# Keys and slots of chunk pairs by seven products, and weight sums kept in DRAM, in a float32 macaron block

## The chip, the cores and the metric

The kernel runs on one core of a Trainium2 chip. The metric is device time in microseconds of one execution. The profile is of one further execution of the same program; its times are counted from the start of its span.

The engines are called TensorE (PE in the profile), VectorE (DVE), ScalarE (ACT), GpSimd (POOL) and SyncE (SP). Each works through its own instructions in order. SP's queue issues nearly all transfers here, one behind the other; POOL's queue issues the indirect ones.

## The reference

The input is 2 batches of 1024 tokens with 512 features, all in float32. A mixture of two experts, an attention with slots and the mixture again are each added to the tokens:

```python
x = x + 0.5 * _L0_ffn_ref(_layernorm(x), w_router, w_fc, w_proj)
x = x + _L0_attn_ref(_layernorm(x), Wq, Wk, Wv, Wg, Ws, Wo, g_norm_weight)
x = x + 0.5 * _L0_ffn_ref(_layernorm(x), w_router, w_fc, w_proj)
# mixture: the router picks one of 2 experts for each token;
#   h = x @ w_fc[e].T  (2048 wide);  a = square(where(h >= 0, h, h / 2));  a @ w_proj[e].T * weight
# attention, 16 heads, 64 slots a head:
#   q, k = x @ Wq, x @ Wk (64 a head);  v, g = x @ Wv, x @ Wg (128 a head)
#   s = clip(x @ Ws, -32, 32);  z = cumulative logsumexp of s over the tokens;  p = exp(s - z)
#   hk = hk * exp(z_before - z) + k p^T;  ok = q hk;  u = softmax(ok)
#   hv = hv * exp(z_before - z) + p v^T;  o = u hv
#   o = o * rsqrt(mean(o^2) + eps) * g_norm_weight * silu(g);   o @ Wo
```

## The kernel before, in words

**Stages.** The first mixture runs from 0 to about 505 us, attention to about 1940, the last mixture to the end. A scheduler orders each engine's instructions and sets the semaphores. Tiles come from pools: `large` has 11 buffers of 8 KB in each partition and holds expert weights, attention weights and tokens; `sums` has 6 buffers of the same size. A load waits until an older tile's buffer is free, and everything behind it on SP's queue waits too.

**Mixture.** Tokens are sorted by expert through DRAM, then worked on in six passes of 2, 4, 2, 4, 1 and 4 tiles of 128 tokens (the last mixture: 4, 4, 4, 2, 2, 1). A pass takes the hidden layer in four quarters (`ck`), each with 1 MB of `w_fc` (tile `wfc`, L223) and 1 MB of `w_proj` (`wp`). The passes of four tiles use Strassen's seven products (matmuls L588 and L653); for these POOL makes sums of the weights, `S` (L538 to L541) and `R` (L550 to L553). The small passes multiply directly (L499 and L708), and there POOL only has its scatter transfers (L628). Finished tokens are scattered to DRAM by POOL's queue.

**Attention.** There are 2 batches × 4 groups of 4 heads × 8 chunks of 128 tokens = 64 units. Three neighbouring units are in work at a time, called `cur`, `mid` and `old`. For `cur` the loop projects keys and slots: `keys_slots` multiplies the chunk with `[Wk | Ws]` in four matmuls of 512 columns (L862) into one PSUM bank; ScalarE copies the key half (L871), VectorE clips the slot half (L873), ScalarE takes its exponential (L874). Then keys and slots are transposed (`tk`, L953 and L954), copied to `kET`, and the scores `Ap` computed (L966). VectorE masks them into `A` (L970), makes the running sum `CT` (L983) and its reciprocal `rC` (L988). In the next step of the loop `ok` uses `A` (L995 and L1000), and on it hang the softmax, the slot weights `Bp`, the output `ov`, the norm with a root on ScalarE (L1075), POOL's gating (L1079) and the output projection `po` (L1113). ScalarE's root and exponential need different tables, which it loads in between.

**Values and gates** of a pair of chunks already come from seven products (`values_gates`, L888), spread over the loop in four steps by `project_ahead`. The token sums `X` of the pair are made by VectorE (L905 to L908). The weight sums `G` are made by POOL in `group_sums` (L846 to L852), eight operations for each batch and group, during the units of the group before. One of the weights is overwritten by its sum.

**Weights.** `group_weights` and `value_gate_weights` load 1 MB each of `wks`, `wv`, `wg`, `wo` and 0.5 MB of `wq` for each batch and group.

## Time and profile before

| | |
|---|---|
| median of 3 runs | 2412.27 us (2410.39 to 2414.95) |
| the profiled execution's own time | 2413.41 us |
| its span | 2411.5 us |
| its mean granted TensorE clock | 0.994 |
| TensorE busy | 2350.5 us (97%) |
| VectorE, ScalarE, POOL busy | 1343.7, 757.7, 488.3 us |
| keys and slots, L862 | 512 passes of 128x512 |
| values and gates, L888, and `hU`, L588 | 10% and 6% of the chain that ended last |

Busy times come from the page. A float32 matmul is recorded as two passes, so four matmuls of a unit are eight records. The recorded duration of a pass includes an end that is modelled, and neighbouring passes overlap; how fast the stream runs is read from the distance of the starts in the timeline. "idle before" in a group's row is the idle time of that engine just before it, with the one that ended it. In the list of waits the numbers are us in total, how many times, and the longest.

### The profile page before, as it was taken

The page shows a single profiled execution, that of the slowest core. Times are in us where ns is not written, and L with a number is a line of the kernel's source. Part 1 is how long each engine was busy: PE and PEld are TensorE (multiplying, and loading weights), DVE is VectorE, ACT ScalarE, POOL GpSimd, SP SyncE. Part 2 cuts the span into 40 slices and gives each one's busy share as a digit, 9 for nine tenths or more (in the row PEclk, how much of TensorE's full clock was granted, in tenths as well). Part 3 has the DMA queues.
Part 4 walks back from the last instruction along what each step waited for, and adds up shares of the span by engine and source line. Part 5 has one row for each costly group of instructions (what it writes and reads, how often), then busy time and mean ns, then how long its engine had stood idle before and what let it go on. Part 6 is the DMA issues. An engine that isn't in the chain of part 4 may idle for free.

```text
span 2411.5 us, 27003 instructions
## 1 busy us (share of the span) xinstructions
PE 2350.5 (97%) x10168; PEld 1497.3 (62%) x10168; DVE 1343.7 (56%) x3020; ACT 757.7 (31%) x1408; POOL 488.3 (20%) x415
## 2 busy tenths in 40 slices
PE   6899999999999999999999999999999999999998
PEld 5587787855555555555555555555555568888865
DVE  5553455665645545556655645645646666766411
ACT  1222222223333333334433333333333332222222
POOL 3522415400100100100201100100102223644000
PEclk9999999999999999999999999999999999999999
DMA  7614335130100100100310100100001113313442
GB/s 262 232 53 178 109 111 204 56 143 1 62 18 1 62 18 1 49 22 14 109 37 36 47 33 1 47 32 1 26 1 53 53 53 122 137 62 131 157 170 96
DMA packets 37601, 180.66 MB, mean 75 GB/s; under 512 B 4575, under 2 KB 4575, under 8 KB 21088
## 3 DMA queue, kind: packets, MB, share of 16 engines
q1 hardware_dynamic: 31904, 161.58, 18.6%
q0 software_dynamic: 5280, 16.85, 1.8%
q8 instruction: 80, 1.31, 0.2%
q10 hardware_dynamic: 288, 0.52, 0.1%
q14 instruction: 49, 0.40, 0.1%
HBM read 160.50 MB, written 18.95 MB: 74 GB/s over the span
## 4 chain that ended last, share of the span: by engine, by line
PE 85%; DVE 7%; issue 4%; DMA 1%; POOL 1%; ACT 1%; SPq 0%; POOLq 0%; ACTq 0%; DVEq 0%
PE U L888 10%; PE po L1113 9%; PE pks L862 9%; PE oa L653 7%; PE hU L588 6%; PE o L653 5%; PE pq L944 5%; PE V L888 4%; PE hp L499 4%; PE op L708 3%; PE hV L588 3%; PE ok L1000 3%; PE C L888 2%; PE ok L995 2%; PE ov L1064 2%
## 5 line engine op out<-in xcount | busy, mean ns | idle before, releaser
L1079 POOL TENSOR_TENSOR sg<-sg,ms 128x512 f32<-128x512 f32 x64 | 67.7, 1058 | 1167.7 <-DVE ms L1077 1143.0
L862 PE MATMUL pks<-wks,xnT 128*128 128x512 f32 x512 | 264.9, 623 | 0.0
L1113 PE MATMUL po<-wo,oT 128*128 128x512 f32 x512 | 231.2, 593 | 1.0 <-ACT oT L1106 1.0
L499 PE MATMUL hp<-xsT,wfc 128*128 128x256 f32 (+1 forms) x768 | 150.9, 352 | 7.5 <-DVE t L486 4.4
L1113 PEld LDWEIGHTS po<-wo,oT 128*128 128x128 f32 x512 | 92.0, 190 | 92.9 <-issue 90.4
L499 PEld LDWEIGHTS hp<-xsT,wfc 128*128 128x128 f32 x768 | 128.6, 193 | 31.0 <-issue 10.0
L708 PE MATMUL op<-wp,a 128*128 128x512 f32 x320 | 143.2, 593 | 0.0
L1118 DVE TENSOR_TENSOR x<-po,x 128x512 f32<-128x512 f32 x64 | 44.2, 691 | 151.5 <-PE po L1113 151.5
L486 DVE SCALAR_TENSOR_TENSOR t<-hp,r 128x256 f32<-128x256 f32 (+1 forms) x96 | 36.3, 378 | 155.6 <-ACT r L485 152.2
L862 PEld LDWEIGHTS pks<-wks,xnT 128*128 128x128 f32 x512 | 83.0, 190 | 54.9 <-issue 46.2
L944 PE MATMUL pq<-xnT,wq 128*128 128x512 f32 x256 | 112.5, 592 | 0.0
L988 DVE RECIPROCAL rC<-CT 128x256 f32<-128x256 f32 x64 | 111.7, 1745 | 0.3
L588 PE MATMUL hU<-xsT,wfc 128*128 128x256 f32 x384 | 101.4, 386 | 2.0 <-ACT e L595 2.0
L895 ACT COPY u<-U 128x512 f32<-128x512 f32 x64 | 37.2, 581 | 197.0 <-PE U L888 197.0
L708 PEld LDWEIGHTS op<-wp,a 128*128 128x128 f32 x320 | 59.7, 190 | 60.9 <-issue 57.4
L1075 ACT ACT_TABLE_LOAD x59 | 75.7, 1283 | 61.8 <-DVE ms L1074 61.6
L871 ACT COPY k<-pks 128x256 f32<-128x256 f32 x64 | 23.8, 372 | 191.3 <-PE pks L862 183.2
L588 PEld LDWEIGHTS hU<-xsT,wfc 128*128 128x128 f32 x384 | 73.2, 193 | 16.0 <-issue 3.3
L1064 PEld LDWEIGHTS ov<-v,B 128*128 128x128 f32 x512 | 76.5, 191 | 10.1 <-issue 3.3
L485 ACT ACTIVATE r<-hp 128x256 f32<-128x256 f32 (+1 forms) x96 | 33.3, 347 | 156.2 <-PE hp L499 153.7
L925 ACT COPY v<-U 128x512 f32<-128x512 f32 x32 | 18.7, 585 | 201.8 <-PE U L888 201.8
L874 ACT ACT_TABLE_LOAD x63 | 80.8, 1283 | 1.1
(277 smaller groups left out, 4947.5 us busy)
## 6 DMA issues: line engine op xcount, KB each, us to landing
wfc<-in_w_fc_dram SPq DMA_DIRECT2D x48, 1024.0 KB, 4.9
wp<-in_w_proj_dram SPq DMA_DIRECT2D x48, 1024.0 KB, 6.5
wv<-in_w_v_dram SPq DMA_DIRECT2D x8, 1024.0 KB, 4.9
wg<-in_w_g_dram SPq DMA_DIRECT2D x8, 1024.0 KB, 4.9
wks<-in_w_ks_dram SPq DMA_DIRECT2D x8, 1024.0 KB, 4.8
wo<-in_w_o_dram SPq DMA_DIRECT2D x8, 1024.0 KB, 4.8
xs<-xs SPq DMA_DIRECT2D x6, 1032.0 KB, 7.0
wq<-in_w_q_dram SPq DMA_DIRECT2D x8, 512.0 KB, 3.6
```

Of the source, the lines that this page charges most:

```text
L499: m.mark = nc.tensor.matmul(hp, lhsT=wfc[:, dc * HQ + hc * P : dc * HQ + (hc + 1) * P], rhs=xT[:, dc, :], start=(dc == 0), stop=(dc == DC ...
L588: m.mark = nc.tensor.matmul(bank, lhsT=left[:, d, :], rhs=right[:, d, :], start=start and d == 0, stop=d == 1, skip_group_check=True,)
L653: nc.tensor.matmul(bank[:, t, :], lhsT=left(q)[:, ts(t, P)], rhs=right(q), start=first and q == 0 and (t == 0 or last), stop=last and q == ...
L708: nc.tensor.matmul(ops[j], lhsT=a[hc][:, ts(j, P)], rhs=wp[:, ts(hc, D)], start=(ck == 0 and hc == 0), stop=(ck == NHQ - 1 and hc == HQ // ...
L862: nc.tensor.matmul(pj, lhsT=xT[u.blk][:, dc, ts(u.c % 4, P)], rhs=w[:, ts(dc, 512)], start=(dc == 0), stop=(dc == DC - 1),)
L874: nc.scalar.activation(u.E, u.E, AF.Exp)
L888: nc.tensor.matmul(bank, lhsT=left[:, d, :], rhs=right(d), start=start and d == 0, stop=d == 1, skip_group_check=True,)
L944: nc.tensor.matmul(pj, lhsT=u.wq[:, c0 : c0 + P], rhs=xT[u.blk][:, dc, :], start=(dc == 0), stop=(dc == DC - 1),)
L988: nc.vector.reciprocal(u.rC, u.CT)
L1064: nc.tensor.matmul(op[:, h, :], lhsT=u.Bm[:, h % 2 * NPR + pr, :], rhs=u.v[:, ts(h, DV)], start=(u.c == 0), stop=(u.c == 0 or h % 2 == 1),)
L1075: nc.scalar.activation(ms, ms, AF.Sqrt, bias=eps, scale=1.0 / DV)
L1113: nc.tensor.matmul(pj, lhsT=u.oT[:, h, :], rhs=u.wo[:, ts(h, D)], start=(h == 0), stop=(h == HG - 1),)
```

## The change

*Keys and slots* are now computed for two chunks together. With the tokens as the left 2x2 block matrix (two chunks by two halves of the features) and the weights as the right one (two halves of the features by keys and slots), seven products of 256 columns take the place of eight. `keys_slots` is a generator: five products in the first step of an even unit, one each in its second and third (`next(keys)`). Two halves `U` and `V` of one PSUM bank (`kU`) accumulate, and one product has a bank of its own (`kC`). The partial results are copied by ScalarE and added by VectorE. The token sums are those of the values (`token_sums`). `project_ahead` for the values moves to odd units, with its last two of five steps in even ones; its `V` products come earlier.

*Weight sums* for values and gates (four operations for each group and half) and for keys and slots (four for each group) are made once, by POOL, in the first mixture's small passes (`weight_sums`, five or ten of its steps within a quarter). They are loaded for that, stored to DRAM (`vg_sums`, `ks_sums`) and loaded in attention for each batch and group like weights, in the units `c` = 4 to 7 of the group before. `group_sums` is gone.

*The tile of blank rows* moves from a constant to a sum tile, set in each mixture. *The last mixture* loads its first tokens before its first `wfc`, and its first `wp` after their preparation (`load_outer`).

```diff
-            self.wp0 = load_expert(w_proj, self.ex[0], 0, f"wp{ph}_0_0")
-            self.raw0 = self.load_tokens(0)
+            if self.split:
+                self.wfc0 = load()
+                self.load_outer()
+                self.raw0 = self.load_tokens(0)
+            else:
+                self.raw0 = self.load_tokens(0)
+                self.wfc0 = load()
...
+        def weight_sums(self):
+            G = nc.gpsimd
+            def sums(b11, b12, b21, b22, T):
+                G.tensor_tensor(T[:, 0], b12, b11, ALU.subtract)
+                yield
+                G.tensor_tensor(T[:, 1], b22, T[:, 0], ALU.subtract)
+                yield
+                G.tensor_tensor(b12, b22, b12, ALU.subtract)
+                yield
+                G.tensor_tensor(T[:, 2], b21, T[:, 1], ALU.subtract)
+                yield
+            def store(to, T, t3):
+                nc.sync.dma_start(out=to[:, 0:2], in_=T[:, 0:2])
+                nc.sync.dma_start(out=to[:, 2], in_=t3)
+                nc.sync.dma_start(out=to[:, 3], in_=T[:, 2])
+            done = None
+            for g in range(NG):
+                for d in range(2):
+                    w = large_tile([P, 4, 512], f"gw{g}_{d}")
...
+                    if done:
+                        store(*done)
+                    T = sum_tile([P, 3, 512], f"G{g}_{d}")
+                    yield from sums(w[:, 0], w[:, 2], w[:, 1], w[:, 3], T)
...
+        def load_values_gates(self, b, g):
...
+            wv = load_w(w_v[g], f"wv{nm}").rearrange("p (k d n) -> p k d n", k=2, d=2)
+            for h in range(2):
+                T.append(large_tile([P, 2, 2, 512], f"vgT{h}_{nm}"))
+                nc.sync.dma_start(out=T[h], in_=sums[:, h])
...
+        def product(bank, left, right, start):
+            for d in range(2):
                 nc.tensor.matmul(
+                    bank, lhsT=left[:, d], rhs=right[:, d],
+                    start=start and d == 0, stop=d == 1, skip_group_check=True,
                 )
-        def keys_slots(u):
-            pj = project_tokens(u, u.wks, "pks")
-            u.k = work.tile([P, HG * DK], F32, tag="k", name=f"k{u.nm}")
-            nc.scalar.copy(u.k, pj[:, 0 : HG * DK])
-            u.E = work.tile([P, HG * M], F32, tag="E", name=f"E{u.nm}", bufs=3)
-            nc.vector.tensor_scalar(u.E, pj[:, HG * DK :], -32.0, 32.0, ALU.max, ALU.min)
-            nc.scalar.activation(u.E, u.E, AF.Exp)
+        def keys_slots(u):
...
+            bank = ps2.tile([P, 2, 256], F32, tag="pj", name=f"kU{u.nm}")
+            U, V = bank[:, 0], bank[:, 1]
+            def keep(bank, tag):
+                t = work.tile([P, 256], F32, tag=tag, name=f"{tag}{u.nm}", bufs=1)
+                nc.scalar.copy(t, bank)
+                return t
...
+            def slot(v, bank, other):
+                v.E = work.tile([P, HG * M], F32, tag="E", name=f"E{v.nm}", bufs=3)
+                nc.vector.tensor_tensor(v.E, bank, other, ALU.add)
+                nc.vector.tensor_scalar(v.E, v.E, -32.0, 32.0, ALU.max, ALU.min)
+                nc.scalar.activation(v.E, v.E, AF.Exp)
+            product(U, a11, B11, True)
+            p1 = keep(U, "kp")
+            C = ps2.tile([P, 256], F32, tag="pj", name=f"kC{u.nm}")
+            product(C, a12, B21, True)
+            nc.vector.tensor_tensor(key(u), C, p1, ALU.add)
+            product(V, u.S[:, 0], T1, False)
+            p5 = keep(V, "kv")
+            product(U, u.S[:, 1], T2, False)
+            u2 = keep(U, "ku")
+            product(V, u.S[:, 3], B22, False)
+            slot(u, V, u2)
+            yield
+            product(U, u.S[:, 2], T3, False)
+            slot(pair[1], U, p5)
+            yield
+            product(U, a22, T4, False)
+            nc.scalar.copy(key(pair[1]), U)
+            yield
...
             if cur:
-                keys_slots(cur)
+                if i % 2:
+                    project_ahead(i)
+                else:
+                    keys = keys_slots(cur)
+                    next(keys)
...
+        many = 1 if ps == 0 and ck == 3 else (0, 0, 2, 0, 1, 0)[ps] if ck < 3 else 0
+        for _ in range(many):
+            next(weight_steps, None)
```

## The prediction

> **What bounds the kernel now.** First the page's busy times and its chain of work that ended last, with the costliest groups.
>
> ```profile
> PE 2350.5 (97%) x10168; PEld 1497.3 (62%) x10168; DVE 1343.7 (56%) x3020; ACT 757.7 (31%) x1408; POOL 488.3 (20%) x415
> PE 85%; DVE 7%; issue 4%; DMA 1%; POOL 1%; ACT 1%; SPq 0%; POOLq 0%; ACTq 0%; DVEq 0%
> L862 PE MATMUL pks<-wks,xnT 128*128 128x512 f32 x512 | 264.9, 623 | 0.0
> L846 POOL TENSOR_TENSOR G<-wg,wv 128x512 f32<-128x512 f32 x16 | 20.9, 1307 | 30.0 <-DMA wg<-in_w_g_dram 30.0
> ```
>
> TensorE is busy 97% of a 2411.5 us span. `pks` (keys and slots) never waits: 0.0 us idle before its 512 passes. Second, the windows view: columns are busy us (and counts) by engine, granted clock, DMA share, GB/s.
>
> ```profile
> 72.00:92.00 20.00, 18.43 (x72) 11.54 (x71) 6.63 (x13) 5.65 (x13) 8.32 (x7) 1.00 0.99 393
> 185.00:255.00 70.00, 70.00 (x286) 52.12 (x285) 28.56 (x52) 16.93 (x41) 23.76 (x20) 1.00 0.48 175
> 540.00:1140.00 600.00, 598.38 (x2553) 318.58 (x2553) 340.87 (x798) 211.91 (x344) 61.16 (x53) 1.00 0.07 25
> 1140.00:1860.00 720.00, 715.97 (x3063) 381.66 (x3062) 414.52 (x989) 256.64 (x415) 84.25 (x76) 1.00 0.10 35
> ```
>
> In attention's steady part TensorE idles 5.6 of 1320 us, at clock 1.00, with DMA nearly empty. Matmul columns taken out there are time, if nothing new makes TensorE wait. The first mixture is different: it has stretches where DMA is full (share 0.99 at 393 GB/s). Third, what TensorE waits for, in the list of waits:
>
> ```profile
> PE rp L284 <- DVE e L275: 12.5, 1, 12.5
> PE ok L995 <- DVE A L970: 8.4, 15, 4.3
> PE hC L588 <- DVE hA L604: 6.4, 2, 3.3
> ```
>
> Last the timeline of TensorE, because mean durations (623 ns) hold the pipeline's modelled end. What counts is start to start.
>
> ```profile
> 223.16 7.07 PE L499 MATMUL hp<-xsT,wfc 128*128 128x256 f32 x32
> 230.07 7.03 PE L708 MATMUL op<-wp,a 128*128 128x512 f32 x16
> ...
> 236.94 1.89 PE L499 MATMUL hp<-xsT,wfc 128*128 128x256 f32 x8
> ```
>
> 32 passes of 256 columns take 230.07 − 223.16 = 6.91 us, 0.216 each; 16 of 512 take 6.87 us, 0.429 each. A pass costs by its columns. (A float32 matmul shows as two passes.)
>
> **Part 1: keys and slots by seven products.** Per pair of chunks, out: 2 chunks × 4 matmuls × 2 passes = 16 passes of 512, 16 × 0.429 = 6.87 us. In: 7 products × 2 matmuls × 2 passes = 28 passes of 256, 28 × 0.216 = 6.05 us. Saved 0.82 to 0.86 us (1/8 of the columns); over 32 pairs 27 us; I take −27.5 (32 × 0.86). Here a rule speaks against the change: the Trainium skill, "TensorE: Matmul & The Clock Gate", section "Back-to-back issue gap", says that in a stream of weight load and matmul the spacing is set by both, and gives 81 ns at 128 columns and 131 at 512, so that it shrinks far less than the columns. Interpolated (an estimate from that page), 256 columns would cost 98/131 = 0.75 of 512, not 0.5: 28 × 0.75 × 0.429 = 9.0 us per pair instead of 6.87, a loss of 2.1 × 32 = 68 us. The rows above are this kernel's own stream in float32, every pass with its weight load (190 ns, inside 216), and they halve exactly. I go by the row.
>
> Around the products, per pair: VectorE gets three more adds of 128x256 (one key, two slots; the same size takes 0.42 us at L970), 1.3 us; ScalarE four copies for two, +0.74 us (0.372 at L871). A pair lasts some 45 us (32 of them from about 505 to 1940), where VectorE is busy 57% and ScalarE 35%: beside TensorE. Without the cover it would be 32 × 2.0 = 64 us. The token sums are those the values already make.
>
> What is new on the path is order. The U and V halves of the keys lie in one bank, so each product but the first ones waits for a read of that bank (ScalarE copy 0.37, with the hand-over some 0.6, an estimate). In the changed program's order I walked an even unit: transposes, a product of 256 (0.86, covers the 0.6 copy of kET), scores `Ap`, 1.3 us of products, half of `ok`, 1.7 us of products, the other half. Before, the second mask (after the first and a 1.74 reciprocal) ends 3 us after `Ap`; the other half of `ok` comes here at 3.6, behind as many columns as the four `pks` passes before it. The table load for the root (1.28 us) lies between the copies of p1 and p5, and the p5 copy is then done at about +4.5 us while the next product on the bank is due at +4.9. From there on 1 to 3 us of other work separates the products. So no stall, by some 0.4 us at the tightest; bounds −2 (POOL's sums, which slow VectorE, leave these windows) to +13 (0.4 us a pair); I take +1.
>
> **Part 2: weight sums.** Removed: 8 groups × 8 POOL operations, rows L846 to L852 together 82.8 us. No TensorE wait hangs on them (they appear in no line of the waits), so their removal is worth nothing by itself. In attention each group now loads 5.25 MB instead of 3 (without wq, wo): the 2.25 MB more are 5.7 us at 393 GB/s in a group of 179 us, and by the changed order each load is released about two units before its use. Cost 0; without that cover 8 × 5.7 = 46 us.
>
> Added in the first mixture: 12 units of 4 POOL operations, 48 × 1.3 = 62 us, 12 MB of loads and 12 of stores (36 transfers), all on SP's one queue. POOL has the room: its timeline shows nothing but four scatters from 151 to 227. The danger is SP's order: a store waits for POOL, and behind it stand later weights.
>
> ```profile
> 188.92 0.33 SPq L223 DMA_DIRECT2D wfc<-in_w_fc_dram  x1
> ...
> 206.17 0.33 SPq L223 DMA_DIRECT2D wfc<-in_w_fc_dram  x1
> ```
>
> Pass 0 to 1: gw0_0 lands at about 83.5 (4 MB queued from 70.8 at 393 GB/s), four sums end at 88.7, the store goes at 89.3 and only then pass 1's first wfc (72.7 before). With 4.9 us to landing and the store ahead it is there at 94.9; the new TensorE order wants it at 94.3, and the first of its Strassen sums (1.26) about 0.4 late. +1.5, bounds 0 to +5.
>
> Pass 2: the third quarter's wfc (188.92 before, first used at 223.16) now stands behind the stores of four units. gw2_1's buffer comes free when pass 1's last projection has used its weights, about 209; it lands at 214, and its four sums (5.2) share POOL with four scatters (4 × 1.28): 223 to 224.5. So wfc goes at about 223, lands at 228 to 229.5, for a use at 223.2 to 224.9: +4.5, bounds +2.6 to +8. Next late would be the fourth quarter's (206.17 before, used 236.94); it goes out near 235 to 238, and as its use moves along, nothing more is lost. Bandwidth: before this stretch moved 70 us × 175 GB/s = 12.2 MB; 13 MB are added: 25.2 MB, at the row's 393 GB/s 64 of 70 us. The Trainium skill, "DMA: Bandwidth & Descriptors", section Specifications, puts the HBM limit per core near 358 GB/s: 70.4 us, no slack at all, and some 6 us more by the time bursts are counted. The row of this chip (393) decides, the other goes into the range.
>
> Pass 4 (three key units): the late wfc lands at 370 and 378 for uses at 373 and 382: +0.5, bounds 0 to +5.
>
> **Part 3: the ends.** At attention's start POOL's group sums no longer slow VectorE (a 3.6 us wait of TensorE lies there), but 5 MB of weights stand ahead of some token loads: −1, bounds −4 to +5. At its end, the last unit has no key products left to cover its masks (before, the last `pks` stood there and TensorE still waited 4.3 us, as VectorE was late); now 0.75 for kET and about 3.5 for the masks are bare: +1.5, bounds −1 to +4. The last mixture's tokens go ahead of its first wfc, and wp after the preparation; before, wfc was issued at 1891 and used at 1943, wp at 1907 and used at 1975: cover of 50 us and more, 0. The memset (0.52 on POOL) hides beside it.
>
> **Sum.** −27.5 + 1.5 + 4.5 + 0.5 − 1 + 1 + 1.5 = −19.5 on the span of 2411.5: 2392. That execution took 2413.41 with 1.9 around the span; the median of the runs shown is 2412.27, so 2412.3 − 19.5 = 2392.8: **2393 us**, −0.8%.
>
> **Rivals.**
> - *The sums' queue costs more.* If wfc in pass 2 lands 10 us later (the page's 358 GB/s with bursts) and pass 0 and 4 go to their upper bounds (+8), the time is 2393 + 14 to 18 = 2408. For it: share 0.99 at 72–92. Against: the walk leaves DMA gaps. Still faster by 0.2%, just.
> - *Slower: the single bank stalls TensorE in every pair.* Place: the products on the kU bank in even units. Price: a table load (1.28 us, twice per unit on ScalarE) that falls before the copy of p1 or p5 makes the next product 1.28 − 0.4 = 0.9 late: 29 us over 32 pairs for one of the copies, 57 for both. It decides from 19.5/32 = 0.6 us per pair on. For it: my slack is 0.4 us and ScalarE's order puts both loads among these copies. Against: ScalarE is only 35% busy. Time: 2422 with one, 2450 with both, between them 2436.
> - *256-column passes don't halve* (the page's rule): 2412 + 68 + 8 = 2488. Against it: 6.91 us for 32.
> - *Better:* sums all hidden and VectorE relieved: 2412 − 27.5 − 2 = 2382.
>
> **How the numbers follow.** Forecast 0.53 (own range 2384 to 2402), better 0.10, costlier queue 0.17, single bank 0.18, no halving 0.02. The measurement tells 0.2% (5 us) from no change. Faster: 0.53 + 0.10 + three quarters of 0.17 = 0.76; same: 0.05; slower: 0.19. Leaving out the lowest 0.05 and about 0.13 at the top: 2380 to 2424.
>
> **What would show it.** Right: key products 0.216 apart, 28 per pair; attention's span shorter by about 26; TensorE waits on wfc of 1 to 8 us in 90–100 and 222–232; no POOL sums after 480. Wrong: waits of the key products on ScalarE's copies above 0.6 us per pair, `ok` waiting for `A` in many units instead of few, or a first mixture that ends more than 12 us later.

## The result, and the profile after

The changed kernel takes **2436.62 us** (median of 4 runs, 2435.84 to 2437.40), the kernel before 2412.24 beside it: a ratio of 1.010, 95% interval 1.0083 to 1.0118. It is 24 us slower, where 19.5 us less were predicted. The profiled execution took 2437.35 us, its span is 2435.6, its mean granted clock 0.988.

The page of the changed kernel, its busy times, its chain, and two groups of instructions:

```profile
PE 2348.2 (96%) x10552; PEld 1574.2 (65%) x10552; DVE 1379.1 (57%) x3116; ACT 788.5 (32%) x1472; POOL 472.4 (19%) x401
PE 81%; DVE 9%; issue 4%; DMA 2%; POOL 1%; ACT 1%; SPq 1%; POOLq 0%; DVEq 0%; ACTq 0%
L511 PE MATMUL hp<-xsT,wfc 128*128 128x256 f32 (+1 forms) x768 | 155.2, 358 | 23.9 <-DMA wfc<-in_w_fc_dram 10.7
L921 PE MATMUL kU<-ksT,X 128*128 128x256 f32 x384 | 106.1, 393 | 0.0
```

TensorE has nearly the busy time of before (2350.5), in spite of an eighth fewer columns for the keys. The mixture's plain products `hp` now wait, for a transfer first of all. `kU` itself shows no idle time; what it costs its neighbours does not stand in its own row. The list of waits of the changed kernel (us in total, times, longest):

```profile
PE hp L511 <- DMA wfc<-in_w_fc_dram: 10.7, 4, 5.1
PE hp L511 <- DVE t L498: 9.9, 5, 4.4
...
PE ok L1091 <- DVE A L1066: 6.0, 19, 1.1
```

And three of the stretches of the windows view that were shown of before (busy us and counts of PE, PEld, DVE, ACT, POOL; granted clock, DMA share, GB/s):

```profile
185.00:255.00 70.00, 61.66 (x237) 45.64 (x236) 28.60 (x43) 12.31 (x31) 40.36 (x32) 0.95 0.81 290
540.00:1140.00 600.00, 597.40 (x2724) 349.92 (x2723) 342.52 (x825) 226.72 (x374) 27.01 (x26) 1.00 0.11 39
1140.00:1860.00 720.00, 715.87 (x3285) 420.98 (x3284) 423.33 (x1045) 270.95 (x448) 41.87 (x42) 1.00 0.14 48
```

In pass 2 (185 to 255) TensorE, busy all 70 us before, idles 8.3 us, and its clock is 0.95. Attention's steady part looks as full as before: its idle time is 6.7 us, as against 5.6. Busy time cannot tell whether the work got shorter there. For that I compare the same places of the program in both timelines: the start of the first matmul of a kind. `tk` is the transposing of a unit's keys; units 4 to 60 hold 28 of the 32 pairs.

| start of (us) | before | after | difference | step of the stretch before it |
|---|---|---|---|---|
| pass 1, first `hU` | 91.7 | 95.3 | +3.6 | +3.6 |
| pass 2, first `hp` | 190.3 | 194.0 | +3.7 | +0.1 |
| pass 4, first `hp` | 350.6 | 371.9 | +21.3 | **+17.6** |
| pass 4, fourth quarter | 380.4 | 411.8 | +31.4 | **+10.1** |
| pass 5, third quarter | 441.5 | 474.7 | +33.2 | +1.8 |
| attention, first product | 501.0 | 529.2 | +28.2 | −5.0 |
| `tk` of unit 4 | 602.6 | 632.6 | +30.0 | +1.8 |
| `tk` of unit 60 | 1873.2 | 1889.0 | +15.8 | **−14.2** |
| last mixture, ninth `hU` | 1958.9 | 1981.7 | +22.8 | **+7.0** |
| last mixture's last quarter of `hp` | 2385.3 | 2409.5 | +24.2 | +1.4 |

The first mixture loses 33 us where 6.5 were predicted. Attention's steady part gains 14 where 24 were predicted (28 × 0.86), and half of that is given back at its end.

### The profile page after: what moved, and what is told of

Same layout as the page of the kernel before. It is cut to its first block, busy times and chain, and to the rows that moved or that the text cites. A ratio compares the mean times of both kernels' runs of the same rounds, so it can differ in the third digit from the quotient of the medians.

```text
span 2435.6 us, 28229 instructions
## 1 busy us (share of the span) xinstructions
PE 2348.2 (96%) x10552; PEld 1574.2 (65%) x10552; DVE 1379.1 (57%) x3116; ACT 788.5 (32%) x1472; POOL 472.4 (19%) x401
## 4 chain that ended last, share of the span: by engine, by line
PE 81%; DVE 9%; issue 4%; DMA 2%; POOL 1%; ACT 1%; SPq 1%; POOLq 0%; DVEq 0%; ACTq 0%
PE U L921 10%; PE po L1209 9%; PE kU L921 7%; PE oa L665 6%; PE hU L600 6%; PE o L665 5%; PE V L921 5%; PE pq L1040 5%; PE hV L600 3%; PE hp L511 3%; PE ok L1096 3%; PE C L921 2%; PE op L720 2%; PE ov L1160 2%; PE ok L1091 2%
## 5 line engine op out<-in xcount | busy, mean ns | idle before, releaser
L511 PE MATMUL hp<-xsT,wfc 128*128 128x256 f32 (+1 forms) x768 | 155.2, 358 | 23.9 <-DMA wfc<-in_w_fc_dram 10.7
L921 PE MATMUL U<-vgT,X 128*128 128x512 f32 x256 | 125.5, 593 | 0.3 <-DVE X L937 0.3
L921 PE MATMUL kU<-ksT,X 128*128 128x256 f32 x384 | 106.1, 393 | 0.0
L960 ACT ACTIVATE th<-sg 128x512 f32<-128x512 f32 x64 | 40.3, 630 | 178.7 <-DVE sg L958 178.5
L921 PEld LDWEIGHTS kU<-ksT,X 128*128 128x128 f32 x384 | 68.3, 189 | 31.3 <-DVE E L1007 9.5
L1195 DVE TENSOR_TENSOR sv<-svp,sv 64x256 f32<-64x256 f32 x96 | 40.5, 422 | 83.2 <-PE svp L1185 81.2
L497 ACT ACTIVATE r<-hp 128x256 f32<-128x256 f32 (+1 forms) x96 | 33.2, 346 | 161.8 <-PE hp L511 159.4
L1202 ACT ACTIVATE oT<-to,gnh 128x512 f32<-128x512 f32 x64 | 43.6, 682 | 124.4 <-PE to L1200 123.9
L600 PEld LDWEIGHTS hU<-xsT,wfc 128*128 128x128 f32 x384 | 73.1, 193 | 16.3 <-issue 2.8
```

The source lines that it names most:

```text
L511: m.mark = nc.tensor.matmul(hp, lhsT=wfc[:, dc * HQ + hc * P : dc * HQ + (hc + 1) * P], rhs=xT[:, dc, :], start=(dc == 0), stop=(dc == DC ...
L600: m.mark = nc.tensor.matmul(bank, lhsT=left[:, d, :], rhs=right[:, d, :], start=start and d == 0, stop=d == 1, skip_group_check=True,)
L921: nc.tensor.matmul(bank, lhsT=left[:, d], rhs=right[:, d], start=start and d == 0, stop=d == 1, skip_group_check=True,)
```

## The experiments

All differences are against the changed kernel unless "before" is named. The time of before in the four sets of runs lay between 2412.4 and 2414.9; a ratio is always to the runs of before on the same chip.

### Whether the sums, or the products, cost the time

*No sums in the first mixture* (no_sums). The weight sums are left out altogether: nothing is loaded, summed or stored for them, and attention loads plain weights in their place, with the same bytes.

```diff
-                nc.sync.dma_start(out=T[h], in_=sums[:, h])
+                nc.sync.dma_start(out=T[h], in_=raw[h])
...
-        many = 1 if ps == 0 and ck == 3 else (0, 0, 2, 0, 1, 0)[ps] if ck < 3 else 0
-        for _ in range(many):
-            next(weight_steps, None)
```

> The changed kernel without the weight sums in the first mixture: no loads for them, no POOL operations, no stores; attention loads plain weights of the same size in their place (so the sums are left out of the computation). If the first mixture's loss (its last hidden product starts 33 us later than before, the first attention product 28 us) is all due to these sums, attention starts 26 to 32 us earlier and the time is 2405 to 2411 us. If part of the loss has another cause (the blank rows' place, the order of the first loads), it stays above 2418.

Measured: 2402.31 us, 0.9959 of before (0.9943 to 0.9975), 34 us less than the changed kernel and a little below the expectation. Attention's first product is at 493.9, 35 us earlier than in the changed kernel. Pass 2 is whole again, in the windows view of this run:

```profile
185.00:255.00 70.00, 70.00 (x280) 51.02 (x279) 26.86 (x50) 16.53 (x40) 24.71 (x20) 1.00 0.50 179
```

The steady part lasts 1256.0 us from unit 4 to 60 (changed kernel 1256.4, before 1270.6). So what the first mixture lost is the sums' doing, all of it, and the products' gain in attention is the small one of the changed kernel with or without them.

*Seven products with POOL's sums in attention* (keys_attn_sums). Nothing in DRAM: `group_sums` stays as before, and POOL makes the keys' sums too. The first step of the last mixture comes two units later, as the sums' buffers ask for it.

```diff
-    weight_steps = att.weight_sums()
...
+                if mid.c == 6 and mid.n + NC < n:
+                    v = units[mid.n + NC]
+                    with tc.issue_after(mid.gated.ins):
+                        for _ in att.key_sums(v.b, v.g):
+                            pass
```

> Keys and slots by seven products as in the change, but every weight sum made by POOL in attention, for each batch and group, eight operations as before and four more for the keys; nothing kept in DRAM. If the products alone give the 0.5 us per pair that the steady part of attention shows (14 us over 28 pairs) less 6 to 10 us at attention's two ends, the time is 2402 to 2410 us. If they give the full column saving of 0.86 us per pair, it is 2385 to 2392. If POOL's sums beside attention slow VectorE enough to stall TensorE, it is above 2412.

Measured: 2418.47 us, 1.0024 (1.0016 to 1.0033). The first mixture is that of before (attention's first product at 500.9). The steady part gains 7.0 us over 28 pairs, and attention's end loses 7.4. A time above 2412 was expected for the case that POOL's sums stall TensorE. The products with POOL's sums beside them, without any of DRAM's costs, are no gain.

*Direct keys* (direct_keys). The changed kernel, with keys and slots by four matmuls of 512 columns for each chunk; they stand first in each unit, and the values keep their five steps.

```diff
-                else:
-                    keys = keys_slots(cur)
-                    next(keys)
+                keys_slots(cur)
```

> The changed kernel with keys and slots as before (four matmuls of 512 columns a chunk), while all weight sums are still made in the first mixture and stored (those of the keys unused). If the seven products save 0.5 us a pair net of the ends, the time is 2442 to 2452 us. If they save nothing, it stays at 2434 to 2440.

Measured: 2454.82 us, 1.0175 (1.0157 to 1.0194), above both expectations. The steady part is 11.0 us *longer* than before's, with the same columns. It cannot be the loads of sums, as the next run shows: with the same loads, and the same columns in another order, its steady part is 19 us shorter. The order of the products is worth nearly as much as the 24 us that their columns were to save.

*The sums alone* (sums_only). Direct keys in the order of before, values and gates in their four steps of before; only the weight sums are made early and loaded (the keys' sums too, which nothing uses).

```diff
-        for _ in range(3):
+        for _ in range(2):
             project_ahead(-1)
...
             if cur:
-                if i % 2:
-                    project_ahead(i)
                 keys_slots(cur)
```

(The diff is to the run with direct keys, and leaves out the four steps themselves, which are the lines of before.)

> Keys and slots by four matmuls of 512 columns per chunk, in the order of the kernel before, and values and gates in their four steps of before; only their weight sums are made in the first mixture (keys' sums too, unused) and loaded from DRAM. If the changed order of products is what cost time in the run with direct keys (steady part 11 us longer than before over 28 pairs), the steady part here is as before or up to 13 us shorter (no POOL sums there), and the time is 2412 + 33 (first mixture) - 5 (attention's start) - 0 to 13 = 2427 to 2440. If the loads of sums cost it, not the order, the steady part is again 11 us longer and the time is about 2450 to 2455.

Measured: 2437.80 us, 1.0092 (1.0077 to 1.0108). This is the time of the changed kernel: **taking the whole of part 1 out of it changes nothing.** Its steady part is 8.1 us shorter than before's, without one column less, though the prediction priced the removal of POOL's sums from attention at nothing. The list of waits of this run:

```profile
PE ok L1053 <- DVE A L1028: 3.7, 5, 2.3
```

Before it was 8.4 us in 15 waits, one of 4.3 us at attention's end. By units, the gain lies in four of eight: from `tk` to `tk`, the units 2, 3, 5 and 6 of a group took 20.57, 22.20, 22.20 and 20.68 us before, and 20.10, 21.99, 21.99 and 20.10 here (means of two groups). POOL's sums stood in the units 3 to 6, so they cannot be the whole of it: unit 2 had none of them and gains, unit 4 had two and doesn't. With POOL's sums gone the scheduler has laid TensorE's own instructions differently in just these four units. Unit 10 (the unit 2 of its group) before, and here:

```profile
742.35 1.12 PE L862 MATMUL pks<-wks,xnT 128*128 128x512 f32 x2
743.68 0.49 PE L995 MATMUL ok<-qT,sk 128*128 128x128 f32 x2 [0.21 <-DVE A L970]
```

```profile
769.26 1.98 PE L983 MATMUL pks<-wks,xnT 128*128 128x512 f32 x4
771.09 0.38 PE L1053 MATMUL ok<-qT,sk 128*128 128x128 f32 x2
```

Four passes of the keys instead of two now cover the mask `A` before `ok`. The units 2 and 6 that were laid so gain 5.2 of the 8.1 us. The units 3 and 5 gain 2.5; there POOL's sums did slow VectorE. Of the token sums `X` of the steady part, 12 ran beside a sum of POOL and took 1.42 us on average, where those beside none took 0.42; with the sums alone, none takes longer than 0.43. Before, in the timelines of POOL and VectorE:

```profile
768.52 1.27 POOL L848 TENSOR_TENSOR G<-wg,G 128x512 f32<-128x512 f32 x1
768.59 1.48 DVE L905 TENSOR_TENSOR X<-X,xnT 128x256 f32<-128x256 f32 x1
```

The softmax behind it on VectorE comes late, and `tu` with it, by 0.2 us.

### Where the products' gain went

With the run of the sums alone beside the changed kernel, the columns of one group of eight units (counted from the timeline's forms) can be set against its times. A column is 0.216/256 us. Units 0 and 4 are the same in both, 25.09 and 26.80.

| from `tk` of unit to the next | columns, sums alone | after | us, sums alone | after |
|---|---|---|---|---|
| 1 | 25088 | 24064 | 21.99 | 21.59 |
| 2 | 23040 | 23040 | 20.10 | 20.42 |
| 3 | 25088 | 24064 | 21.99 | 21.88 |
| 5 | 25088 | 24064 | 21.99 | 21.71 |
| 6 | 23040 | 23040 | 20.10 | 20.42 |
| 7 | 23552 | 22528 | 20.86 | 20.94 |

The columns save 4 × 1024, or 3.44 us in the group, as the prediction had it (0.86 a pair). The group's time falls by 0.07 us. The other 3.37 us are small gaps. Here is the start of interval 3 in the changed kernel's timeline of TensorE:

```profile
791.03 0.72 PE L1062 MATMUL Ap<-qT,kET 64*128 64x128 f32 x8
791.69 0.70 PE L921 MATMUL kC<-wks,xnT 128*128 128x256 f32 x2
792.72 0.49 PE L1091 MATMUL ok<-qT,sk 128*128 128x128 f32 x2 [0.33 <-DVE A L1066]
```

The timeline of VectorE in the same place:

```profile
792.24 0.42 DVE L1066 TENSOR_TENSOR A<-Ap,causal 128x256 f32<-128x256 f32 x1
```

And the same place with the sums alone:

```profile
788.71 0.72 PE L1024 MATMUL Ap<-qT,kET 64*128 64x128 f32 x8
789.36 1.13 PE L983 MATMUL pks<-wks,xnT 128*128 128x512 f32 x2
790.39 0.49 PE L1053 MATMUL ok<-qT,sk 128*128 128x128 f32 x2
```

Between the scores `Ap` and the first half of `ok` stood two passes of 512 columns, 1.03 us from start to start. Now there are two of 256, half the cover, and `ok` still starts 1.03 us after them, because it waits for the mask. The gap between `kC` and `ok` is 0.43 us longer than the one between `pks` and `ok`, 17 times in the steady part: 7.4 us. A further 4.8 us lie between `to` and `kU` (27 × 0.18), where `kU` starts 0.05 us after ScalarE's copy of the bank has ended. Interval 2 has no key product and no wait on the list, and still 0.32 us more. There `ok` and `tu` start 0.07 and 0.09 us later than the columns ask, each 0.05 us after what it needs has ended on VectorE (the mask) or ScalarE (`e`), and the pass behind each is late by another 0.10 and 0.06 us. These waits are too short for the list. The mask and `ok` in the changed kernel's timelines:

```profile
950.67 0.42 DVE L1066 TENSOR_TENSOR A<-Ap,causal 128x256 f32<-128x256 f32 x1
951.15 0.49 PE L1091 MATMUL ok<-qT,sk 128*128 128x128 f32 x2
```

Here too, two passes stand between `Ap` and `ok` where the old order had four.

*Two banks* (two_banks). The halves of the keys get a PSUM tile each.

```diff
-            bank = ps2.tile([P, 2, 256], F32, tag="pj", name=f"kU{u.nm}")
-            U, V = bank[:, 0], bank[:, 1]
+            U = ps2.tile([P, 256], F32, tag="pj", name=f"kU{u.nm}")
...
-            product(V, u.S[:, 0], T1, False)
+            V = ps2.tile([P, 256], F32, tag="pj", name=f"kV{u.nm}")
+            product(V, u.S[:, 0], T1, True)
```

> The changed kernel with the V products of the keys in a PSUM tile of their own instead of the second half of the U bank. The gap of about 0.19 us between the output transposes and the next key product (25 pairs of the 28 looked at) should go, if it is the wait for ScalarE's copy out of the shared bank: 4 to 6 us faster than the change, 2431 to 2433. If it is the switch between kinds of matmul, no change: 2435 to 2438.

Measured: 2438.64 us, 1.0111 (1.0094 to 1.0128): no gain. The gap of 0.19 us is still there: the product waits for ScalarE's copy out of its own bank instead (0.05 us after `kv` ends). So the single bank does not set the time. The rival that named 2436 us for it met the number by luck.

*The products one place later* (swap_slots). In even units the values' fourth product goes first and the key products come after it.

```diff
-                if i % 2:
-                    project_ahead(i)
-                else:
-                    keys = keys_slots(cur)
-                    next(keys)
+                project_ahead(i)
```

> The changed kernel with the values' fourth product ahead of the key products in even units, and the key products one place later. The steady part of the changed kernel has 25 us fewer columns than the run with the sums alone, and 19 us more waiting. If the waits come of where the short key products stand (7.4 us of them between the second key product and ok, 4.8 between to and a key product), the steady part is 8 to 12 us shorter than the changed kernel's and the time 2425 to 2429. If the masks come late whatever stands before them, the steady part is within 3 us of the changed kernel's: 2434 to 2440.

Measured: 2434.61 us, 1.009 (1.0071 to 1.0108). The steady part is 1.9 us shorter than the changed kernel's, or 0.7 to 0.8 us a group in full groups. The expectation of 8 to 12 us fails: the gaps between `kC` and `ok` and before `kU` are gone, but others of the same kind appear, behind `U` above all. Most of the loss is not tied to one place.

*Sums later in the unit, two banks, and the last pair's products later* (together). From the run with POOL's sums in attention; `issue_after` names the unit's `uT` instead of its gating (the edit shown; the two others are those of the run with two banks and of the next run).

```diff
-                    with tc.issue_after(mid.gated.ins):
+                    with tc.issue_after(mid.turned.ins):
```

> Keys and slots by seven products with all weight sums made by POOL in attention and nothing in DRAM; the halves of the keys in banks of their own; the sums issued after the unit's uT instead of after its gating; the last pair's last two products of keys and of values one unit later. If POOL's sums beside the masks took the half of the gain that the run with sums in attention lacked (7 of 14 us), and the bare last unit another 3 to 5, the time is 2418 - 7 - 4 = 2407, between 2402 and 2411. If POOL's sums cost VectorE the same wherever they stand, 2414 to 2418.

Measured: 2424.40 us, 1.0041 (1.0027 to 1.0054), above both expectations. The steady part is only 1.1 us shorter than before's, worse than with the sums after the gating (7.0). The three edits together help nothing; which of them harms was not tried.

*The last pair's products later* (late_last). The last two products of keys and of values go from unit 62 to unit 63.

```diff
+                if i == n - 1:
+                    next(last)
...
+                elif i == n - 1:
+                    next(last)
+                    next(keys)
```

> The changed kernel with the last two products each of keys and of values and gates of the last pair moved from unit 62 to unit 63, which has no products of its own. If attention's end (5 to 7 us lost between unit 60 and the last mixture) is missing cover in unit 63, the time is 2430 to 2433. If it is VectorE's load there, it stays at 2435 to 2438.

Measured: 2435.77 us, 1.0101 (1.0085 to 1.0118): no difference that can be told. From `tk` of unit 60 to the last mixture's `hU` it takes 92.2 us as against 92.7. Moving products does shift time between the last two intervals (27.21 and 17.55 us become 22.45 and 21.81), but takes none away. The end's loss lies one unit earlier: the interval from unit 60 to 61 took 26.34 us before and 32.32 after. There the last mixture's routing stands among attention's work, and TensorE idles 3.4 us in it (2.5 of them before `tu`, for ScalarE's `e`), where it idled 0.0 before. The windows view from unit 60 to the last mixture's ninth `hU`, of the changed kernel and of before:

```profile
1889.00:1981.70 92.70, 81.15 (x362) 48.84 (x361) 58.44 (x136) 30.62 (x48) 27.17 (x24) 0.91 0.21 74
```

```profile
1873.20:1958.90 85.70, 77.89 (x350) 43.24 (x349) 55.03 (x133) 27.91 (x46) 21.45 (x18) 0.98 0.18 68
```

TensorE idles 11.6 us there instead of 7.8, and the granted clock is 0.91 instead of 0.98: some 8 us of clock lost instead of 1.7. So what the end loses are waits and the slower clock with them. What makes the routing collide more than before was not tried. The run with the sums alone loses 2.6 us between unit 60 and the last mixture, the changed kernel 7.0.

### What of the sums is late in the first mixture

*Stores on POOL's queue* (pool_stores).

```diff
-                nc.sync.dma_start(out=to[:, 0:2], in_=T[:, 0:2])
+                nc.gpsimd.dma_start(out=to[:, 0:2], in_=T[:, 0:2])
```

> The changed kernel with the stores of the weight sums issued on POOL's own queue instead of SP's. Same bytes. If the order on SP's queue is what costs (weights of the next quarter standing behind stores that wait for POOL), most of the 28 to 33 us come back: 2408 to 2420 us. If the 24 MB themselves fill the transfers, it stays at 2428 to 2440.

Measured: 2439.62 us, 1.0119 (1.0096 to 1.0142). Pass 1 starts at 91.7 as before, so there it was the store ahead of the weights on SP's queue. But by pass 4's fourth quarter 27.6 of the 31.4 us are lost again: pass 1 now loses 7.1, from pass 2's start to pass 4's it is 11.0 us instead of 17.6, and within pass 4 9.5 instead of 10.1. The stores' place in SP's queue is at most a part of what is lost in pass 2, and hardly any in pass 4.

*No stores* (no_stores) and *no operations of POOL* (no_pool_sums). The first loads and sums but stores nothing, and attention loads plain weights. The second loads and stores the plain weights and leaves the sums out. Both thus compute attention with other weights.

```diff
-                nc.sync.dma_start(out=to[:, 0:2], in_=T[:, 0:2])
-                nc.sync.dma_start(out=to[:, 2], in_=t3)
-                nc.sync.dma_start(out=to[:, 3], in_=T[:, 2])
+                pass
...
-                G.tensor_tensor(T[:, 0], b12, b11, ALU.subtract)
-                yield
+                for _ in range(4):
+                    yield
```

(The first four changed lines are the one run's, the last four the other's.)

> The changed kernel with the loads and POOL's sums in the first mixture, but without the stores of the sums; attention loads plain weights of the same size (so the sums are left out of the result). Without any sums the time was 2402 us, with all of it 2437. If the stores (12 MB, and the weights that stand behind them on SP's queue) are the cost, 2402 to 2412. If the loads of 12 MB and POOL's work are, 2422 to 2437.

> The changed kernel with the loads and the stores in the first mixture, but the four POOL operations of each unit left out: the loaded weights are stored (so the sums are left out of the result). Stores wait for the loads alone. If waiting for POOL, and POOL's slowing of VectorE, is the cost, 2402 to 2415. If the 24 MB through one queue are the cost by themselves, 2425 to 2437.

Measured: 2424.86 us, 1.0045 (1.0031 to 1.006), with single runs from 2419 to 2434; and 2420.52 us, 1.003 (1.0018 to 1.0041), between the two expectations. Beside the 2402 without anything and the 2437 with all: loads and POOL cost 23 us, loads and stores 18, all three 34. No one part is the cause, and each of the two pairs loses more than half of the whole. With loads and stores but no POOL, DMA itself is full, in the windows view of the run without POOL's operations:

```profile
190.00:225.00 35.00, 35.00 (x144) 26.86 (x142) 16.16 (x32) 7.13 (x18) 3.91 (x4) 1.00 1.01 359
```

*Whole rows* (wide_loads). The weights to be summed are loaded in rows of 8 KB for each partition instead of two halves in rows of 2 KB, two whole weights for one group.

```diff
-                    w = large_tile([P, 4, 512], f"gw{g}_{d}")
-                    for i, src in enumerate((w_v, w_g)):
...
+                wv, wg = load_w(w_v[g], f"gv{g}"), load_w(w_g[g], f"gg{g}")
```

> The changed kernel with the weights to be summed loaded whole, in rows of 8 KB per partition, where it loads two halves in rows of 2 KB; the same bytes, sums and stores. If the short rows slow the transfers, the loads land in 5 to 6 us where they took 8 to 11, the third quarter's wfc of pass 2 goes before 226, the loss in pass 2 falls from 18 us to under 8 and the time to about 2425. If the bytes themselves, POOL and the order of the queue set it, the loss stays within 4 us of the changed kernel's: 2433 to 2441.

Measured: 2448.68 us, 1.0135 (1.012 to 1.0151), slower than both expectations. From pass 2's start to pass 4's it loses 20.6 us, as against 17.6: short rows are not what makes it late. Pass 1 loses 10.7 us as well, where the changed kernel loses next to nothing. I had not thought of POOL there: pass 1 needs its own sums `S`, which now stand behind eight of the added ones in a row, and TensorE waits 6.2 us for them.

*Half as many units in pass 2* (spread). A unit is the four sums of one piece of the weights, with its loads and stores. One operation of the sums to a step in pass 2 and two in pass 4, where it was two and one.

```diff
-        many = 1 if ps == 0 and ck == 3 else (0, 0, 2, 0, 1, 0)[ps] if ck < 3 else 0
+        many = 1 if ps == 0 and ck == 3 else (0, 0, 1, 0, 2, 0)[ps] if ck < 3 else 0
```

> The changed kernel with half as many sums at a time in pass 2 (three units there where there were seven) and the rest in pass 4 (eight units where there were four). If the late wfc comes of the number of loads, sums and stores between two of the mixture's own weights, pass 2 loses under 6 us instead of 17.6, pass 4 loses 20 or more instead of 10, and the time is 2430 to 2442. If pass 2 loses the same 18 with half the units, something else is late there, and the time is over 2445.

Measured: 2450.40 us, 1.0156 (1.0138 to 1.0173). From pass 2's start to pass 4's, 1.3 us are lost with three units (17.6 with seven); within pass 4 37.3 us with seven units (10.1 with three; the expectation counts one too many in both). Where they fit the units are nearly free, and each one above that costs about 4 us in pass 2 and 7 in pass 4, which is shorter. Halving pass 2's share moved the loss to pass 4 and doubled it: the time, 2450, is past what I expected. The wait sits where the prediction looked for it, but in the other pass. In this run's timeline of TensorE, in pass 4:

```profile
396.67 6.50 PE L511 MATMUL hp<-xsT,wfc 128*128 128x128 f32 x32 [10.41 <-DMA wfc<-in_w_fc_dram]
```

### A version faster than both

If attention gains some 8 us without POOL's sums, and few of them are free in the first mixture, the products can be left out and the sums be made once, in the gaps.

*Once in attention* (sums_once). The kernel before; POOL's sums of the first sequence are stored, and loaded for the second.

```diff
+    POOLED = {(0, g) for g in range(NG)}
...
+            if (b, g) not in POOLED:
+                for d in range(2):
+                    nc.sync.dma_start(
+                        out=T[d].rearrange("p a b -> p (a b)"), in_=ts_dram[g][:, ts(d, 1536)]
+                    )
```

> The kernel before, with the keys as they were and the first mixture untouched; the weight sums of values and gates that POOL makes for the first sequence are stored and loaded for the second, so POOL makes them in four groups instead of eight. If POOL's sums beside VectorE cost the 8 us that the run with sums alone gained in the steady part (0.29 us a pair), half of that is gained: 2412 - 4 = 2408. If the loads of sums in the run with sums alone gained it otherwise (an earlier load of the other weights), no gain: 2411 to 2414.

Measured: 2410.70 us, 0.9992 (0.9983 to 1.0000). The trace has the gain in the second sequence, 0.94 us a group (180.44 to 179.50), and 1.8 us of loss by attention's start in this execution. As a time it cannot be told from no change. Here the two causes come apart: POOL's sums are gone from the whole second sequence, but the units 6 of its full groups keep the order of before, and take 20.68 us as before; the units 2 have the new order and gain 0.47.

*Two groups in the first mixture* (two_groups). As the last one, and the sums of groups 0 and 1 are made in the first mixture, one operation to a step. (In POOL's order all four units come to lie in pass 2, none in pass 4.)

```diff
+    POOLED = {(0, g) for g in range(2, NG)}
...
+        if ps in (2, 4) and ck < 3:
+            next(early, None)
```

> As the kernel before, with the sums of the first two groups made in the first mixture's passes 2 and 4, one operation to a step (three units of four operations in pass 2, one in pass 4), those of the other two by POOL in attention for the first sequence, and loads for the second. If few units cost the first mixture little, as three in pass 2 did in the run that spread them (1 to 3 us), and POOL's sums cost 0.29 us a pair in six of eight groups and 3 to 5 us at attention's start, the time is 2412 + 2 - 6 - 3 = 2405. If the first mixture loses by any sums at all, 2412 to 2420.

Measured: 2408.02 us (14 runs), 0.9982 of before (0.9974 to 0.9990): 4 us less than before, 29 less than the changed kernel. It is the fastest complete version here, by about as much as a measurement of this kernel can tell. It reaches pass 2 at 187.0 (190.3 before), loses 5.9 us with its four units from there to pass 4, and gains 5.0 from pass 4 to attention's first product, which is at 498.6 (501.0 before). Attention's steady part is 3.0 us shorter, again in the units that the scheduler laid differently. TensorE's list has one wait for `wfc`, of 1.9 us.

## Why the prediction was wrong

**The step that failed most: part 2, pass 2, "wfc goes at about 223".** The mechanism was as told: sums wait for weights, stores for sums, and the third quarter's `wfc` stands behind them. The sizes were not. The changed kernel's timeline of SP:

```profile
203.19 1.38 SPq L862 DMA_DIRECT2D gw<-in_w_g_dram  x1
...
210.73 0.77 SPq L862 DMA_DIRECT2D gw<-in_w_g_dram  x1
...
225.59 0.38 SPq L853 DMA_DIRECT2D vgs<-G  x1
230.60 0.33 SPq L854 DMA_DIRECT2D vgs<-gw  x1
231.81 0.32 SPq L855 DMA_DIRECT2D vgs<-G  x1
232.41 0.34 SPq L223 DMA_DIRECT2D wfc<-in_w_fc_dram  x1
```

The timeline of POOL in the same stretch:

```profile
214.78 1.35 POOL L843 TENSOR_TENSOR G<-gw 128x512 f32<-128x512 f32 x1 [8.80 <-DMA gw<-in_w_g_dram]
...
221.12 1.72 POOL L843 TENSOR_TENSOR G<-gw 128x512 f32<-128x512 f32 x1
223.00 1.26 POOL L640 DMA_INDIRECT x<-xs  x1 [0.16 <-issue]
...
229.29 1.28 POOL L847 TENSOR_TENSOR gw<-gw 128x512 f32<-128x512 f32 x1
```

And that of TensorE:

```profile
222.09 1.99 PE L511 MATMUL hp<-xsT,wfc 128*128 128x256 f32 x8 [1.35 <-DVE t L498]
237.77 9.39 PE L511 MATMUL hp<-xsT,wfc 128*128 128x256 f32 x32 [5.11 <-DMA wfc<-in_w_fc_dram]
```

A unit's load, 203.19, was in use at 214.78: 11.6 us, not the 5 us to landing that the page of before gives for a load on a quiet queue. I took a landing time from a quiet stretch for one in which my own sum had 25 MB in flight. So POOL came to the unit that holds up `wfc` (its last load went at 210.73) at 221.12, where I had 214. Its operations, and those of the unit before it, took up to 1.7 us instead of 1.3, and four scatters went in between (223.00 to 229.29), as foreseen. So `wfc` went at 232.41, 9 us later than predicted. I stopped there: "nothing more is lost". TensorE indeed has no wait on record for the fourth quarter's `wfc`, though it went at 249.29. What I left out is VectorE, which made `hp` wait 3.1 us in pass 2 and `hV` 3.4 us behind it (both for `t`), and the clock: after the stalls the 32 passes at 237.77 took 9.39 us on record where before they took 7.07. From pass 2's start to pass 4's, in the windows view of the changed kernel and of before:

```profile
194.00:371.90 177.90, 161.60 (x662) 126.17 (x661) 86.14 (x130) 38.97 (x92) 87.72 (x67) 0.96 0.55 195
```

```profile
190.30:350.60 160.30, 156.65 (x662) 124.03 (x662) 74.23 (x130) 39.37 (x92) 49.02 (x38) 0.99 0.35 123
```

For the same 662 passes TensorE idles 16.3 us instead of 3.7, and is busy 5.0 us longer at a clock of 0.96 instead of 0.99: these are the 17.6 us, where 4.5 were predicted. In pass 4 it was 10.1 for 0.5; of that, 3.6 us are a wait for `wfc` and 4.3 waits for VectorE. In pass 0 to 1 it was 3.6 for 1.5, within its bounds.

**Bandwidth, row against rule.** I took 393 GB/s from a stretch of `wfc` and `wp` loads, in whole rows, and set aside the figure of the Trainium skill, "DMA: Bandwidth & Descriptors", section Specifications, 358 GB/s for the HBM of a core. With loads and stores of the sums, at shares of 0.97 to 1.01, this chip moved 343 GB/s (200 to 215 in the changed kernel) and 359 (190 to 225 without POOL's operations); 387 were reached once, at 245 to 260. The row I chose was no row of this mix: 393 lies above all three, and the page's 358 lies among them. The rule's price, 70.4 us for 70, was the safer one.

**Part 1: right in columns, wrong in time.** The columns fell by 0.86 us a pair: four passes of `kU` of 256 columns start 1240.96 to 1241.83, 0.217 each, half of 0.429 again, so that the rule on the issue gap that spoke against this does not hold here. But compared with the run of the sums alone, full groups kept 0.07 of 3.44 us, and the steady part as a whole 6.1 of 24 us over 28 pairs (much of that where the second sequence begins). That the steady part came out 14 us shorter is luck in part: 8.1 of them come with the removal of POOL's sums, which was priced at nothing. "What is new on the path is order … I take +1": this term measured some 18 us. In my walk 1.3 us of products stood between `Ap` and the first half of `ok`; the order has one of 256 columns, or only part of it. A narrower product is worse cover for a neighbour that waits for VectorE. My forecast read cover from the idle time of TensorE, and waits of up to 0.2 us stand in no list of it.

**"Removal is worth nothing by itself"** (part 2): wrong, to the good. The steady part is 8.1 us shorter without POOL's sums. Some 2.5 us of it are what I had passed over: no wait of TensorE *named* POOL, but POOL's adds slowed VectorE's token sums from 0.42 to 1.4 us, and TensorE waited for VectorE. Most of the rest, 5.2 us, is not POOL's time at all: the scheduler laid four passes of the keys before `ok` in two units of a group, where two had been. This is the cover of the mask again.

**The ends.** Attention's start gained 5.0 us up to its first product, of which 1.8 are lost again by unit 4: −3.2 for −1, within its bounds. The end lost 7.0 for +1.5, beyond its bound of +4. The bare last unit was the wrong place: late_last gains 0.5 us. Most of the loss lies in the unit with the last mixture's routing, 6.0 us, in waits and in the slower clock; why they come there stays open.

**The rivals.** "The sums' queue costs more" was the right rival, still too small: with its 14 to 18 us on top of the 6.5 the first mixture would have lost 20 to 25, and it lost 33. The single bank's middle case met the time (2436) by luck: waits for ScalarE's copies cost some 0.18 us a pair, where it named 0.9, and the run with two banks is no faster. Of the signs named for "wrong" it was the third that came, a first mixture that ends more than 12 us later; the second, `ok` waiting for `A` in many units, came with waits mostly too short for the list.

## What to carry to other kernels

A transfer's landing time belongs to the load of its stretch: if a change fills the queue, take the time to landing from a full stretch, and follow each later weight on the same queue, not the first one only. Find out how much of a background work fits by trying half of it. Fewer columns are time only where nobody leans on them: look which wait each product covers before narrowing it, and compare the same place of both timelines, since busy time and waits can both look unchanged. And before you credit a gain to the work that was taken out, compare the order of what is left: a scheduler can have changed it.

## What was unexpected of the hardware

- A stall of TensorE costs twice: in the stretch 230 to 245 of the changed kernel TensorE was busy for 9.9 of 15 us and the granted clock was 0.77; the mean clock of the execution fell from 0.994 to 0.988. The Trainium skill, "TensorE: Matmul & The Clock Gate", section "HAM oscillation — how this bites in real kernels", has a rule for it (no gap of TensorE above some 3.4 us). The wait of 5.11 us is above that, but here shorter ones were enough: in the run two_groups the clock was 0.50 from 214.3 to 217.6, just after a wait of 2.31 us. My +4.5 for pass 2 counted no clock.
- Steps between full matmuls and those of 64 rows or columns make the next start 0.09 to 0.10 us later than the columns ask, and are booked as neither idle nor waiting; steps without such a change and without a wait cost 0.00. That a change of the tiling mode drains the array stands in the Trainium skill, "TensorEngine Tiling (Array Packing)", section "Key Properties"; the size is from these runs. The two orders have as many of these steps in interval 2, twelve.
- POOL's sums slowed VectorE's: before, the token sums took 1.42 us on average beside one of them, and 0.42 alone or beside POOL's gating.
- Loads of 0.5 MB took a median of 8.4 and 11.0 us to land (`gw`) in the changed kernel, and 5.9 and 6.7 in the run that spread them, where a load of 1 MB (`wfc`, over the whole execution) had 5.0.
